# Where x is loaded around the projection of a two-layer kernel: three tiles in the last attention head, layer 1's tiles during the projection

## The chip, the cores and the metric

The kernel runs on one core of one Trainium2 chip. The metric is the device time of one execution in microseconds (us), taken as the median over runs. A profile of one further execution, with its hardware trace, is there as well; its instants are us from the start of the span.

## What is computed

The input x is one image of 48 channels and 256 x 256 pixels in float32. Two layers are applied, each with a group norm in front and a residual around it:

```
x = x + L0(groupnorm(x))     # attention over patches
x = x + L1(groupnorm(x))     # channel, column and row mixing in 64 x 64 windows

L0: qkv = 3x3 depthwise conv of (w_qkv applied to the channels)
    patches of 4 x 4, stride 4, padding 4; 8 heads of 96 features
    q, k scaled to unit length; attn = softmax(q k * temperature)
    out = v times attn, folded back to pixels, then w_proj over the channels
L1: out = sum over t < 3 of einsum('bcphqw,twW,thH,tcC->bCpHqW', x in windows, Ws, Hs, Cs)
```

There are 4096 patches inside the image; the padding patches enter the softmax as a constant.

## The kernel before

**Attention.** After a first stage (group statistics, the 1x1 convolution of the first two heads, the depthwise convolution of head 0) one long stretch runs under `tc.manual_schedule()`: each engine gets its instructions in the order of the text. It loops over 8 heads `h` and 16 blocks `g`. In each block PE makes scores (L337), ACT exponentiates them (L566), PE weighs the values (L595, in four parts `k`), and DVE accumulates into `oacc` (L606). While head `h` runs, the `Depthwise` objects prepare head `h + 1`; their tiles (`pad`, `acc`, `o` and others), and those of the strips of the 1x1 convolution, lie in the pool `cv`, about 50 KB a partition. In the last head nothing is left to prepare, but `cv` is held to the end, by `attention.close()`. SP loads the keys, queries and values; `load_query` (L311) fills one of two buffers for the block after next.

`store(h, m)` (L608 to L618) transposes a part of `oacc`, copies it to `oo` on ACT (two buffers, in the pool `asm`), and POOL stores it to `os_` in DRAM. The last head's eight stores are spread over the last block, and the last two come at its very end.

**Projection.** Then a loop over 8 tiles `t` of 16 rows of each half of the image follows, outside the manual schedule, so the order of instructions is planned by the framework. For each tile SP loads `pot` from `os_` (L740) and `pxt`, the same rows of x, from the input (L741), two DMAs of 768 KB each; the two pools have three buffers each. PE applies `wp` (L746), DVE adds into `pxt` (L753) and takes the statistics for the second group norm (L757), and POOL stores `pxt` to `x1s` in DRAM (L762). After the loop, a chain of small operations (L764 to L788) makes `csn` and `cbias` out of the statistics: the channel weights of layer 1 with the norm folded in.

**Layer 1.** A second manual schedule works in units of 64 rows by 128 columns. `load_x(u)` (L815) reads `lxq` from `x1s`, with the channels on partitions; `load_rows(u)` (L824) reads `lrt` from `x1s`, with the rows on partitions, for the residual. `over_c` applies `csn` (L841, DVE writes `lzt` at L848), `over_w` (L863) and `over_h` (L880) follow, and POOL stores the result. The tiles `lxq` lie in the pool `lx` (three buffers), opened after the projection's pools are closed, on the memory that these held. Units 0 and 1 are asked for first thing:

```
for u in range(2):
    load_x(u)
for _ in over_c(0):
    pass
```

Of the kernel before, what the change touches and what calls it, by code (L numbers as in the profile page):

```python
# [8 lines left out]
F32 = mybir.dt.float32  # L9
# [4 lines left out]
PSUM = bass.MemoryType.PSUM  # L14
DRAM = bass.MemoryType.DRAM

C = 48
H = W = 256
HALF = H // 2
P2 = 2 * C  # L20
KS = 4
KK = KS * KS
NH = 8
HD = C * KK // NH
# [9 lines left out]
PX = W // KS  # L34
# [5 lines left out]
TP = 256  # L40
T3 = 3
WS = 64
# [3 lines left out]
def conv_preact_kernel(  # L46
# [15 lines left out]
    nc = tc.nc  # L62
    xc = x.rearrange("b c y x -> (b c) y x")
# [15 lines left out]
    x1s = dram.tile([C, H, W], F32, name="x1s")  # L79
# [18 lines left out]
    for s in range(2):  # L98
        r = slice(s * C, (s + 1) * C)
        for h in range(NH if s == 0 else H0):  # L100
            o = s * M0 + h * HC if h < H0 else (h - H0) * HC
            nc.gpsimd.dma_start(
                out=(wq[r] if h < H0 else wr[0:C])[:, o : o + HC].rearrange("c (z e) -> c z e", z=3),
                in_=w_qkvT.rearrange("c (z h e) -> h c z e", z=3, h=NH)[h],
# [373 lines left out]
                nc.sync.dma_start(out=rows, in_=ot[s * M0 : (s + 1) * M0])  # L478

    attention = ExitStack()  # L480
    cv = attention.enter_context(tc.tile_pool(name="cv", bufs=1))
    one = attention.enter_context(tc.tile_pool(name="one", bufs=2, space=PSUM))

    ots = [cv.tile([M1, 4, W + 2], F32, name=f"ot{i}") for i in range(NOT)]
# [39 lines left out]
    with tc.tile_pool(name="ahead", bufs=2) as ah, tc.tile_pool(name="ae", bufs=3) as ae, tc.tile_pool(  # L524
        name="asm", bufs=6
    ) as asm, tc.tile_pool(name="ao", bufs=1) as ao, tc.tile_pool(name="big", bufs=3, space=PSUM) as big:
        MB = 8
        NK = NB // MB
        NG = NB // G
        keys, queries, values, oaccs = {}, {}, {}, {}  # L530

# [76 lines left out]
        def store(h, m):  # L608

            pt = one.tile([HD, 4, 128], F32, name="pt", tag="one")  # L610
            for i in range(4):
                nc.tensor.transpose(pt[:, i, :], oaccs[h, m // 2][:, m % 2, i * HD : (i + 1) * HD], ident)  # L612
            oo = asm.tile([HD, 512], F32, name="oo", bufs=2)
            nc.scalar.copy(oo, pt.rearrange("p i n -> p (i n)"))  # L614
            for i in range(512 // TP):
                nc.gpsimd.dma_start(  # L616
                    out=os_[m * (512 // TP) + i, h * HD : (h + 1) * HD, :], in_=oo[:, i * TP : (i + 1) * TP]
                )  # L618
# [16 lines left out]
        with tc.manual_schedule():  # L635
            load_query(0, 1)
            block = scores(0, 0)
            for h in range(NH):
                more = h + 1 < NH
                rows = {r: Depthwise(h + 1, r) for r in range(CR + 1)} if more else {}  # L640
                for g in range(NG):
                    p, d, n = rows.get(g - 2), rows.get(g - 1), rows.get(g)

                    if h == 0 and 0 < g <= 6:
                        load_value(0, g + 1)
                    if more and CR + 2 <= g < CR + 6:
                        for m in range(2):
                            load_value(h + 1, (g - CR - 2) * 2 + m)
                    if more and CR + 3 <= g < CR + 6:
                        for m in range(2):  # L650
                            load_key(h + 1, (g - CR - 3) * 2 + m)

                    blocks = [normalised(*block)]
                    if p:
                        p.norm()
                        p.root()
                    block = scores(h, g * G + 1)
                    if more and g == NG - 1:
                        load_key(h + 1, 6)
                        load_key(h + 1, 7, nc.gpsimd)  # L660
                    if g + 2 < NG:
                        load_query(h, g + 2)
                    elif more:
                        load_query(h + 1, g + 2 - NG)
                    if p:
                        p.scale()
                    if d:
                        for t in range(1, 4):
                            d.tap(t)
                    second = block  # L670
                    if g + 1 < NG:
                        block = scores(h, (g + 1) * G)
                    elif more:
                        block = scores(h + 1, 0)
                    blocks.append(normalised(*second))
                    if d:
                        for t in range(4, 9):
                            d.tap(t)

                    if g == 0 and rows:  # L680
                        rows[0].load()

                    if h == 0 and 0 < g <= 6:
                        turn(0, g + 1)
                    if more and CR + 2 <= g < CR + 6:
                        for m in range(2):
                            turn(h + 1, (g - CR - 2) * 2 + m)
                    if g == 0 and h > 0:
                        for m in range(6, 8):
                            store(h - 1, m)  # L690
                    if p:
                        p.patches()
                        p.store((2,))
                        p.high()
                    if d:
                        d.square()
                    if n:
                        n.first()
                    for k in range(NK):
                        s = (h * NG + g) * NK + k  # L700
                        weigh(h, g, blocks, k)
                        if k == 0 and d:
                            d.reduce()
                        if k == 0 and p:
                            p.low(nc.gpsimd)
                            p.store((0, 1))
                        if s % 2:
                            for w in strips[s - 1] + strips[s]:
                                w.run(big.tile([128, 2, 512], F32, name="big"))
                            for w in strips[s + 1] + strips[s + 2]:  # L710
                                w.load()
                        elif s:
                            for w in strips[s - 2] + strips[s - 1]:
                                w.store()
                        if k == 2 and g + 1 in rows:
                            rows[g + 1].load()

                        if g == NG - 1 and k > 0:
                            for m in range(2 * k - 2, 2 * k):
                                store(h, m)  # L720
            for m in range(6, 8):
                store(NH - 1, m)
# [1 line left out]


    l1c = ctx.enter_context(tc.tile_pool(name="l1c", bufs=1))
    RP = TP // PX * KS
    NP = TP
    with tc.tile_pool(name="pj", bufs=3) as pj, tc.tile_pool(name="pjs", bufs=1) as pjs, tc.tile_pool(
        name="pps", bufs=3, space=PSUM  # L730
    ) as pps, tc.tile_pool(name="pp1", bufs=1, space=PSUM) as pp1:
# [1 line left out]
        ov = os_.rearrange("t (c k) n -> t c k n", k=KK)  # L733
        for t in range(HALF // RP):
            ot = pj.tile([P2, KK, NP], F32, name="pot")
            xt = pj.tile([P2, RP, W], F32, name="pxt")
            for s in range(2):
                r = slice(s * C, (s + 1) * C)
                y0 = s * HALF + t * RP
                nc.sync.dma_start(out=ot[r], in_=ov[s * (NT // 2 // TP) + t])  # L740
                nc.sync.dma_start(out=xt[r], in_=xc[:, y0 : y0 + RP, :])  # L741
            xv = xt.rearrange("p (py ki) (px kj) -> p ki kj py px", ki=KS, kj=KS)
            for ki in range(KS):
                ps = pps.tile([P2, KS, NP], F32, name="pps")
# [15 lines left out]
            for s in range(2):  # L760
                y0 = s * HALF + t * RP
                nc.gpsimd.dma_start(out=x1s[:, y0 : y0 + RP, :], in_=xt[s * C : (s + 1) * C])  # L762

        gm2 = pjs.tile([P2, 64 + C], F32, name="gm2")  # L764
        nc.vector.memset(gm2, 0.0)
# [20 lines left out]
        nc.tensor.matmul(pb1, lhsT=mrow, rhs=csn[0:C], start=True, stop=True)  # L786
        cbias = l1c.tile([128, T3 * C], F32, name="cbias")
        nc.vector.tensor_copy(cbias, pb1)  # L788


    with tc.tile_pool(name="lx", bufs=3) as lx, tc.tile_pool(name="lz", bufs=2) as lz, tc.tile_pool(
        name="lr", bufs=2
    ) as lr, tc.tile_pool(name="ly", bufs=4) as ly, tc.tile_pool(name="ps1", bufs=2, space=PSUM) as ps1, tc.tile_pool(
        name="ps2", bufs=2, space=PSUM
    ) as ps2, tc.tile_pool(name="ps3", bufs=1, space=PSUM) as ps3:
        wsb = lz.tile([128, T3, 128], F32, name="wsb", bufs=1)
# [2 lines left out]
        for s in range(2):  # L799
            r = slice(s * WS, (s + 1) * WS)  # L800
            nc.scalar.dma_start(out=wsb[r, :, r], in_=Ws.rearrange("t w v -> w t v"))
            nc.scalar.dma_start(out=hsb[r], in_=Hs.rearrange("t h g -> h t g"))
        HW = WS // 2
        units = [(yw, xh) for yw in range(H // WS) for xh in range(2)]
        NQ = 3
        xqs, rts, zts, blks, parts = {}, {}, {}, {}, {}

        def load_x(u):

            yw, xh = units[u]  # L810
            xcol = slice(xh * 128, (xh + 1) * 128)
            xq = lx.tile([64 + C, HW, 128], F32, name="lxq")
            for s in range(2):
                y0 = yw * WS + s * HW
                nc.sync.dma_start(out=xq[s * 64 : s * 64 + C], in_=x1s[:, y0 : y0 + HW, xcol])  # L815
            xqs[u] = xq

        def load_rows(u):

# [80 lines left out]


        with tc.manual_schedule():
            for u in range(2):
                load_x(u)
            for _ in over_c(0):
                pass
            late = None
# [57 lines left out]
```

## Time and profile before

| | |
|---|---|
| median of 3 runs | 3701.59 us |
| lowest, highest | 3696.06, 3705.06 us |
| profiled execution | 3698.24 us, its span 3696.2 us |
| busy: PE, DVE, ACT, POOL | 94%, 58%, 51%, 15% of the span |
| last head | about 2860 to 3210 |
| last stores of attention, first projection matmul | 3210 to 3239 |
| projection, first matmul to last statistics | 3239 to 3380 |
| statistics chain and wait for layer 1's x | 3380 to 3400 |
| layer 1 | 3400 to 3696 |
| DMA | 386.48 MB, 105 GB/s over the span |

Busy times are of instructions at work; PE's weight loads overlap its matmuls. "SPq" names the DMAs that SP issues, with the time that the issue took. A DMA share of 1 means that the core's 16 DMA engines were all busy. Releasers of waits ("<-") are inferred from semaphore events.

### The profile page before, as it was taken

What the parts mean: (1) busy time and instruction counts of PE and PEld (TensorE: products, weight loads), DVE (VectorE), ACT (ScalarE), POOL (GpSimd) and SP (SyncE); (2) the same over time, 40 slices, a digit from 0 to 9 for tenths busy, and PEclk for the clock granted to TensorE, in tenths of its full rate; (3) what the DMA queues carried; (4) which work ended last, traced back from release to release, by engine and by line L of the source; (5) the groups of instructions that cost most, each with busy time, mean ns of one, the idle gap of its engine ahead of it and who ended that gap; (6) DMA issues with size and microseconds to landing.
All of it is one profiled execution on the core that took longest, in us unless ns stands there. A gap on an engine that the chain in (4) does not pass through costs nothing.

```text
span 3696.2 us, 100318 instructions
## 1 busy us (share of the span) xinstructions
PE 3466.8 (94%) x44252; PEld 2905.8 (79%) x44252; DVE 2139.4 (58%) x3514; ACT 1873.3 (51%) x2747; POOL 542.9 (15%) x628
## 2 busy tenths in 40 slices
PE   2869999999999999999999999999999999855998
PEld 1337777898888898988888989888889888713776
DVE  5454774189628953894399349925982222266654
ACT  0235676566546654665566556655664444300332
POOL 2030111012111211121122112201220000000011
PEclk9989999999999999999999999999999999966999
DMA  7455666533323332333233323332333100299774
GB/s 160 152 133 153 176 170 171 149 96 95 94 79 82 93 89 75 83 90 96 73 92 86 87 73 93 86 87 84 94 79 87 36 19 19 51 248 197 127 138 92
DMA packets 274146, 386.48 MB, mean 105 GB/s; under 512 B 77010, under 2 KB 211522, under 8 KB 269480
## 3 DMA queue, kind: packets, MB, share of 16 engines
q1 hardware_dynamic: 234790, 264.95, 27.4%
q0 software_dynamic: 35424, 106.40, 12.4%
q10 hardware_dynamic: 3490, 8.64, 1.1%
q8 instruction: 350, 5.73, 0.7%
q14 instruction: 92, 0.75, 0.1%
HBM read 234.76 MB, written 144.90 MB: 103 GB/s over the span
## 4 chain that ended last, share of the span: by engine, by line
PE 82%; DMA 6%; DVE 2%; issue 1%; SPq 1%; ACT 1%; ACTq 0%; POOL 0%; POOLq 0%; DVEq 0%
PE big L337 36%; PE big L595 35%; PE pb L863 4%; PE pa L841 2%; PE pc L880 2%; DMA pxt<-in_x_dram 2%; DMA t<-ot 1%; PE big L177 1%; DVE acc L228 1%; PE pt L612 1%; DMA pad<-t 1%; PE pn L247 1%; DMA pot<-os__70 1%; PE pst L549 1%; DMA x1s<-pxt 0%
## 5 line engine op out<-in xcount | busy, mean ns | idle before, releaser
L566 ACT ACTIVATE e<-big,nmx 128x1024 f32<-128x1024 f32 x1024 | 1143.8, 1118 | 875.5 <-PE big L337 613.1
L337 PE MATMUL big<-kt,qt 128*128 128x512 f32 x6144 | 1436.7, 392 | 31.1 <-DMA kt<-qkv 29.0
L595 PEld LDWEIGHTS big<-vn,e 128*64 128x64 f32 x32768 | 1357.0, 137 | 57.2 <-ACT e L566 30.6
L595 PE MATMUL big<-vn,e 128*64 128x96 f32 x32768 | 1387.3, 247 | 6.1 <-DVE oacc L606 2.5
L337 PEld LDWEIGHTS big<-kt,qt 128*128 128x128 f32 x6144 | 1144.6, 188 | 279.6 <-issue 28.8
L606 DVE TENSOR_TENSOR oacc<-big,oacc 128x768 f32<-128x768 f32 x480 | 453.4, 954 | 713.0 <-PE big L595 713.0
L228 DVE SCALAR_TENSOR_TENSOR acc<-pad,dwt,acc 126x1024 f32<-126x1024 f32 x592 | 765.5, 1293 | 39.8 <-ACT acc L209 24.0
L295 POOL DMA_DIRECT2D qkv<-o x72 | 52.8, 734 | 1240.7 <-ACT o L279 1240.7
L579 DVE TENSOR_REDUCE zt<-zs 128x1 f32<-128x4 f32 x256 | 38.4, 150 | 335.1 <-ACT e L566 335.1
L289 POOL TENSOR_TENSOR ol<-o,oh 126x1024 fp32r<-126x1024 f32 x78 | 184.9, 2370 | 311.1 <-DVE ss L243 237.8
L566 ACT ACTIVATION_READ_ACCUMULATOR e<-big,nmx 128x1 f32 x1024 | 196.3, 192 | 0.0
L848 DVE TENSOR_TENSOR lzt<-pa,cbias 128x864 f32<-128x864 f32 (+1 forms) x88 | 137.0, 1628 | 96.4 <-PE pa L841 96.4
L870 ACT COPY lyt<-pb 128x512 f32<-128x512 f32 x144 | 84.5, 587 | 212.4 <-PE pb L863 212.4
L279 ACT COPY o<-acc 126x1024 f32<-126x1024 f32 x74 | 159.1, 2150 | 0.0
L863 PEld LDWEIGHTS pb<-wsb,lzt 128*64 128x64 f32 x2304 | 126.1, 138 | 27.6 <-issue 19.5
L616 POOL DMA_DIRECT2D os__70<-oo x128 | 65.2, 515 | 541.6 <-ACT oo L614 541.3
L863 PE MATMUL pb<-wsb,lzt 128*64 128x128 f32 x2304 | 142.0, 279 | 1.3 <-issue 1.3
L746 PE MATMUL pps<-pot,wp 96*96 96x512 f32 x128 | 79.1, 787 | 61.5 <-DMA pot<-os__70 61.5
L239 ACT ACTIVATE sq<-acc 126x1024 f32<-126x1024 f32 x74 | 78.2, 1057 | 100.7 <-DVE acc L228 100.7
L180 ACT ACTIVATE ot<-big,bias 108x1024 f32<-108x1024 f32 x64 | 68.2, 1111 | 113.1 <-PE big L177 71.4
L209 ACT ACTIVATE acc<-pad,dwt 126x1024 f32<-126x1024 f32 x74 | 84.1, 1137 | 80.6 <-DMA pad<-t 80.6
L746 PEld LDWEIGHTS pps<-pot,wp 96*96 96x96 f32 x128 | 26.9, 219 | 113.3 <-issue 79.0
(124 smaller groups left out, 1977.0 us busy)
## 6 DMA issues: line engine op xcount, KB each, us to landing
pad<-t SPq DMA_DIRECT2D x238, 254.0 KB
t<-ot SPq DMA_DIRECT2D x128, 217.7 KB
qkv<-ol POOLq DMA_DIRECT2D x78, 336.0 KB, 6.1
qkv<-oh POOLq DMA_DIRECT2D x70, 336.0 KB, 5.6
qt<-qkv SPq DMA_DIRECT2D x176, 96.0 KB
xs<-in_x_dram SPq DMA_DIRECT2D x128, 96.0 KB
os__70<-oo POOLq DMA_DIRECT2D x128, 96.0 KB, 2.1
pxt<-in_x_dram SPq DMA_DIRECT2D x16, 768.0 KB
```

Source lines behind the costliest of these rows:

```text
L209: nc.scalar.mul(self.acc, self.pad[:, 0:KS, 0:W], dwt[:, self.h, 0:1])
L228: nc.vector.scalar_tensor_tensor(self.acc, self.pad[:, dy : dy + KS, dx : dx + W], dwt[:, self.h, tap : tap + 1], self.acc, ALU.mult, ALU.add,
L279: nc.scalar.copy(self.o.rearrange("p (a b) x -> p a b x", a=KS), self.acc.rearrange("p a (x b) -> p a b x", b=KS))
L289: eng.tensor_sub(self.ol, self.o, self.oh.bitcast(F32))
L337: nc.tensor.matmul(ps[:, i, :], lhsT=qt[:, r, q0 : q0 + 128], rhs=kts[2 * j + i][:, r // 2, :], start=(r == 0), stop=(r == 2),)
L566: nc.scalar.activation(e[:, j * 1024 : (j + 1) * 1024], ps.rearrange("p a b -> p (a b)"), AF.Exp, bias=nmx[:, b : b + 1], accum_out=zs[:, ...
L595: nc.tensor.matmul(ps[p : p + 64, j // 4, j % 4 * HD : (j % 4 + 1) * HD], lhsT=e[:, mb * 128 + p : mb * 128 + p + 64], rhs=vn, start=(i == 0),
L606: nc.vector.tensor_add(oaccs[h, k], ps[:, :, : 4 * HD], oaccs[h, k])
L746: nc.tensor.matmul(ps[:, i : i + 2, :], lhsT=wp, rhs=ot[:, ki * KS + i : ki * KS + i + 2, :], start=True, stop=True,)
L848: nc.vector.tensor_tensor(zv[:, :, y0 : y0 + n, :], pa[:, :, : n * T3 * C].rearrange("p s (y k) -> p s y k", y=n), cbias.rearrange("p (u v ...
L863: nc.tensor.matmul(pb[s * WS : (s + 1) * WS, i, :], lhsT=zts[u][:, t * C + c + i, :], rhs=wsb[:, t, :], start=True, stop=True,)
L870: nc.scalar.copy(yt[:, t, :], pb.rearrange("p i x -> p (i x)"))
```

## The change

The pool `cv` gets a stack of its own, `convolution`, on the right-hand side of the memory, and is closed at the start of the last head. A pool `pe` takes its place. It holds three tiles `xts` of x, for the projection's tiles 0 to 2, and one more buffer of `oo`, for the very last store. The x tiles are loaded by SP in blocks 1 to 6 of the last head, in the parts k = 1 and k = 3 of each, with two DMAs of 4 rows of a half (192 KB) each time, 24 in all. The projection loads x only for t >= 3.

The pool `lx` is opened ahead of the projection's pools, so it shares no place with them, and `load_x` for units 0 and 1 moves from the head of layer 1 to the end of the projection's loop. `pe` is closed after `cbias`.

```
+    convolution = ExitStack()
+    cv = convolution.enter_context(tc.tile_pool(name="cv", bufs=1, side="right"))
+    NX = 3
...
+            late = h == NH - 1 and m >= NM - NLATE
+            oo = (pe if late else asm).tile([HD, 512], F32, name="oo", bufs=NLATE if late else 2)
...
+                    if not more and g == 0:
+                        convolution.close()
+                        early = ExitStack()
+                        pe = early.enter_context(tc.tile_pool(name="pe", bufs=1, side="right"))
+                        xts = [pe.tile([P2, RP, W], F32, name=f"xt{t}") for t in range(NX)]
...
+                        if not more and 0 < g <= 2 * NX and k in (1, 3):
+                            i = (g - 1) * 2 + k // 2
+                            t, y = i // 4, i % 4 * (RP // 4)
+                            for half in range(2):
+                                y0 = half * HALF + t * RP + y
+                                nc.sync.dma_start(
+                                    out=xts[t][half * C : (half + 1) * C, y : y + RP // 4, :],
+                                    in_=xc[:, y0 : y0 + RP // 4, :],
+                                )
...
+    lx = ctx.enter_context(tc.tile_pool(name="lx", bufs=3))
...
-            xt = pj.tile([P2, RP, W], F32, name="pxt")
+            xt = xts[t] if t < NX else pj.tile([P2, RP, W], F32, name="pxt")
...
-                nc.sync.dma_start(out=xt[r], in_=xc[:, y0 : y0 + RP, :])
+                if t >= NX:
+                    nc.sync.dma_start(out=xt[r], in_=xc[:, y0 : y0 + RP, :])
...
+        for u in range(2):
+            load_x(u)
...
+    early.close()
...
         with tc.manual_schedule():
-            for u in range(2):
-                load_x(u)
             for _ in over_c(0):
```

More of the change, by code (lines that the diff above doesn't have):

```diff
@@ L480, in conv_preact_kernel @@
     attention = ExitStack()
-    cv = attention.enter_context(tc.tile_pool(name="cv", bufs=1))
+    convolution = ExitStack()
+    cv = convolution.enter_context(tc.tile_pool(name="cv", bufs=1, side="right"))
+    NX = 3
     one = attention.enter_context(tc.tile_pool(name="one", bufs=2, space=PSUM))
@@ L528, in conv_preact_kernel @@
         NK = NB // MB
+        NLATE = 1
+        RP = TP // PX * KS
         NG = NB // G
@@ L612, in store @@
                 nc.tensor.transpose(pt[:, i, :], oaccs[h, m // 2][:, m % 2, i * HD : (i + 1) * HD], ident)
-            oo = asm.tile([HD, 512], F32, name="oo", bufs=2)
+            late = h == NH - 1 and m >= NM - NLATE
+            oo = (pe if late else asm).tile([HD, 512], F32, name="oo", bufs=NLATE if late else 2)
             nc.scalar.copy(oo, pt.rearrange("p i n -> p (i n)"))
@@ L726, in conv_preact_kernel, with load_x @@
     l1c = ctx.enter_context(tc.tile_pool(name="l1c", bufs=1))
-    RP = TP // PX * KS
     NP = TP
+    lx = ctx.enter_context(tc.tile_pool(name="lx", bufs=3))
+    HW = WS // 2
+    units = [(yw, xh) for yw in range(H // WS) for xh in range(2)]
+    xqs = {}
+    def load_x(u):
+        yw, xh = units[u]
+        xcol = slice(xh * 128, (xh + 1) * 128)
+        xq = lx.tile([64 + C, HW, 128], F32, name="lxq")
+        for s in range(2):
+            y0 = yw * WS + s * HW
+            nc.sync.dma_start(out=xq[s * 64 : s * 64 + C], in_=x1s[:, y0 : y0 + HW, xcol])
+        xqs[u] = xq
     with tc.tile_pool(name="pj", bufs=3) as pj, tc.tile_pool(name="pjs", bufs=1) as pjs, tc.tile_pool(
@@ L788, in conv_preact_kernel @@
         nc.vector.tensor_copy(cbias, pb1)
-    with tc.tile_pool(name="lx", bufs=3) as lx, tc.tile_pool(name="lz", bufs=2) as lz, tc.tile_pool(
-        name="lr", bufs=2
-    ) as lr, tc.tile_pool(name="ly", bufs=4) as ly, tc.tile_pool(name="ps1", bufs=2, space=PSUM) as ps1, tc.tile_pool(
+    early.close()
+    with tc.tile_pool(name="lz", bufs=2) as lz, tc.tile_pool(name="lr", bufs=2) as lr, tc.tile_pool(name="ly", bufs=4) as ly, tc.tile_pool(name="ps1", bufs=2, space=PSUM) as ps1, tc.tile_pool(
         name="ps2", bufs=2, space=PSUM
@@ L802, in conv_preact_kernel @@
             nc.scalar.dma_start(out=hsb[r], in_=Hs.rearrange("t h g -> h t g"))
-        HW = WS // 2
-        units = [(yw, xh) for yw in range(H // WS) for xh in range(2)]
         NQ = 3
[L806 to L816, printed above, removed]
+        rts, zts, parts = {}, {}, {}
         def load_rows(u):
```

## The prediction

> **What bounds the kernel now.** The page comes first: PE is busy 94% of the span, but its 40 slices dip near the end, and the DMA digits rise to 9 there. The change touches only that stretch, so I read it by windows (columns: length, PE, PEld, DVE, ACT, POOL busy, PE clock, DMA share, GB/s).
>
> ```profile
> DMA  7455666533323332333233323332333100299774
> 2980.00:3040.00 60.00, 60.00 (x786) 53.14 (x784) 13.80 (x34) 28.94 (x48) 0.00 (x0) 1.00 0.08 22
> 3222.00:3239.00 17.00, 3.92 (x39) 3.09 (x35) 0.96 (x1) 4.08 (x7) 6.05 (x12) 0.70 0.80 171
> 3252.00:3272.00 20.00, 10.44 (x16) 3.52 (x16) 17.18 (x20) 0.00 (x0) 2.04 (x4) 0.69 1.01 257
> 3290.00:3308.00 18.00, 10.32 (x16) 3.52 (x16) 12.51 (x12) 0.00 (x0) 1.01 (x2) 0.69 1.00 262
> 3344.00:3362.00 18.00, 9.05 (x16) 3.05 (x16) 12.33 (x12) 0.00 (x0) 1.01 (x2) 0.78 1.01 269
> 3362.00:3380.00 18.00, 10.09 (x16) 3.41 (x16) 12.55 (x13) 0.00 (x0) 1.01 (x2) 0.69 0.45 129
> 3386.00:3393.00 7.00, 0.18 (x1) 0.00 (x0) 0.69 (x2) 0.00 (x0) 0.00 (x0) 0.50 1.18 162
> 3475.00:3510.00 35.00, 35.00 (x500) 26.23 (x492) 21.48 (x15) 10.56 (x18) 4.17 (x6) 1.00 0.79 141
> ```
>
> Three stages show. The last head (row 2980) is PE's alone, DMA at 0.08. The projection (rows 3252 to 3344) is bound by the DMA engines: share 1.0, about 262 GB/s, while PE works 10 and DVE 12.5 of 18 us per tile. In layer 1 (row 3475) PE is full again. Ahead of the projection (row 3222) and behind it (row 3386) PE stands nearly idle; the timeline gives the ends of the second gap:
>
> ```profile
> 3339.57 0.42 SPq L741 DMA_DIRECT2D pxt<-in_x_dram  x1
> 3362.70 10.09 PE L746 MATMUL pps<-pot,wp 96*96 96x512 f32 x16 [9.04 <-DMA pot<-os__70]
> 3379.89 1.88 DVE L130 BATCH_NORM_AGGREGATE mv<-st 96x2 f32<-96x384 f32 x1
> 3384.66 11.16 SPq L815 DMA_DIRECT2D lxq<-x1s  x4
> 3386.22 0.31 DVE L788 COPY cbias<-pb 128x144 f32<-128x144 f32 x1 [0.61 <-PE pb L786]
> 3393.05 0.81 PE L841 MATMUL pa<-csn,lxq 48*128 48x144 f32 x2 [6.87 <-DMA lxq<-x1s]
> 3398.37 3.22 PE L841 MATMUL pa<-csn,lxq 48*128 48x144 f32 x22 [4.50 <-DMA lxq<-x1s]
> 3400.18 3.08 DVE L848 TENSOR_TENSOR lzt<-pa,cbias 128x864 f32<-128x864 f32 x2 [13.01 <-PE pa L841]
> ```
>
> The statistics end at T = 3379.9. cbias is ready 6.6 us later, but DVE's first lzt comes 20.3 us after T, because lxq is asked for only at 3384.66. SP's own waits say why, and one early DVE line shows how the untied part of the program is ordered:
>
> ```profile
> SPq L741 <- DMA x1s<-pxt: 81.2, 5, 22.4
> SPq L815 <- DMA x1s<-pxt: 44.2, 2, 28.1
> SPq L740 <- DMA os__70<-oo: 21.5, 3, 10.9
> 3210.50 0.15 DVE L765 MEMSET gm<- 96x112 f32 x1 [0.64 <-DVE vn L585]
> ```
>
> SP stood 44.2 us in front of lxq for stores of x1s, although unit 0 needs only rows 0 to 63, the first four tiles of one half. It waited for the last tile's stores: for lxq's place, which the projection's pool held. And the memset of L765, written behind the tile loop, ran at 3210, before it: what is ready is put forward.
>
> **What the Trainium skill says.** "DMA: Bandwidth & Descriptors", section "Issuing engines are not separate DMA queues", says that transfers issued by SP, ACT and GpSimd share the same 16 engines. The trace agrees: SP's loads and POOL's stores together fill the share to 1.0. Its "Specifications" give 512 B as enough for line rate; here the measurement decides: lxq and lrt move 512 B pieces (128 columns of f32) and reach 141 to 205 GB/s at a share above 1, the projection's longer pieces 262. "TensorE: Matmul & The Clock Gate", Part 1, says that an idle PE falls to half clock; the trace shows 0.50 from 3380 to 3420. I expect that ramp again, only earlier.
>
> **The change part by part.** One half-tile is 768 KB, so pot, x and the x1s store of a tile are 1.573 MB each.
>
> *x in the last head.* 24 loads of 192 KB over blocks g = 1 to 6. On SP they stand behind load_query(g+2) in each block. A block is 21.8 us; four issues at about 0.41 us (pxt's median) are 1.7 us, and 768 KB at 262 GB/s 2.9 us. From 2830 to 3200 SP spent 271.2 us in 17 waits for PE before query loads, and a query asked for in the middle of block g is needed a block later: of the 21.8 us its nine or so issues of 0.43 us and the landing (2 to 3 us, estimated from the 2.1 of os) take 7, so some 15 are spare. Cost 0; uncovered it would be 4.6 us a block. Their place is that of cv, whose last tenant, head 7's convolution, ended a head earlier. Moving cv itself to the other side costs 0 plus or minus 2 us.
>
> *Start of the projection.* Before, the first x loads (3210) ran against the os stores: the oo copies waited up to 7.0 us for their buffers, and the second half of pot was asked for at 3232.41. The stores' usual landing is 2.1 us. Without x in the way, and with the last oo in its own buffer, m = 4 lands near 3227 and PE begins near 3233 instead of 3238.9. The new lx moves pot over keys and e, last used by 3223, and the later x tiles over oacc and oo, free near 3230: neither is later than pot's data. Gain 6 (2 to 8).
>
> *The DMA-bound middle.* From 3238.9 to the last tile's first matmul at 3362.7 are 123.8 us, for 7 tiles of loads (22.0 MB) and about six tiles of stores (9.4 MB): 254 GB/s. Two x tiles leave this stretch (the first had landed before it): 28.3 MB, 111.4 us. Gain 12.4. With DVE at 12.5 us a tile it stays DMA's.
>
> *Layer 1's loads.* Units 0 and 1 are 3.15 MB. At the 144 GB/s of 3384 to 3407 they cost 21.9 us, at the best windows' 203 GB/s 15.5; I take 18.5. All depends on where they enter SP's queue. They are ready when tile 3 is stored, just when SP stands before the x of tile 6 or 7 for its buffer (the 81.2 us). As L765 went forward, so I expect these four to go in front of the last x loads. Then they take their 18.5 us from the saturated engines before the last tile lands. SP's four issues, up to 5.2 us each in layer 1, hold back the loads behind them, while the engines stay busy.
>
> *The gap.* With lxq there, over_c begins when csn, cbias and the place of lzt are ready. That place is still the projection's and waits for the last x1s store, landed by T + 4.7 before; DVE's wsb memset waits with it. First lzt near T + 8 instead of T + 20.3: gain 12.3 (8 to 13). Behind it nothing changes: over_c(0) at half clock, then PE-bound units; the lrt loads move forward with it.
>
> Sum: 6 + 12.4 - 18.5 + 12.3 = 12.2 us. The profiled execution took 3698.24 (span 3696.2); that leaves 3686.0. The median of the three runs lies 3.35 above it, so 3689.4.
>
> **The rivals.** *A, the lxq loads stay behind the last tile.* They then use the tail, where the share is 0.45. T falls by 18.4; lxq shares the engines with the last x1s store, so lzt starts near T + 10: gain 10. Sum 28.4, median 3673. For it: the order of the text, and x and pot of one tile keep it in the trace. Against: L765.
>
> *B, the change doesn't do what it says:* the waits for x1s are for its data, not for the place, and are not by rows. The trace shows waits by part for os (first pot at 3221.21, later stores from 3222) but cannot tell for x1s. Then only the 18.4 remain: 3683. If instead the 512 B pieces cost 30 us inside the full engines, nothing remains: 3701.
>
> *C, slower: the last head's cover fails.* If the x loads hold the queries back, PE waits in six blocks: 6 x 4.6 = 27.6 us against a gain of 12.2, 15 slower, 3717. It decides once a query lands over 15 us later than now. Against it: heads 0 to 6 run at shares of 0.3 with PE full.
>
> **How the numbers follow.** Forecast 0.56, with a range of its own of 3682 to 3697; A 0.18; B 0.13; C, with any other loss, 0.13. Within 0.3% (11 us, about what a measurement of this kernel can tell from no change) lies a little less than half of the forecast, since 12.2 is barely above it, and B's costly end: 0.30. Faster 0.57, slower 0.13. The range, 3668 to 3708, reaches past A and leaves most of C out.
>
> **What would show it.** Right: PE full from 2920 to 3210 with DMA share near 0.15; four lxq issues before the last pxt; T within 5 us of 3380 and first lzt 8 us after it; no SP wait of L815 at 3340. Wrong: T near 3361 with lxq last (A); lxq after T (B); idle PE in L337 for qt (C).

## The result and the profile after

The changed kernel takes 3677.03 us (median of 4 runs, 3676.36 to 3681.3) against 3703.24 us for the kernel before in the same comparison. The ratio is 0.9934, with a 95% interval from 0.9918 to 0.995: some 24 us, between 18 and 30. The profiled execution took 3676.93 us, its span is 3674.8 us, 21.4 us below the span before.

The page's row of the DMA share, in 40 slices, now shows the last head's x loads as a 2 and a 2 ahead of the empty stretch, and the slices of the projection as 0, 8, 9 instead of 2, 9, 9:

```profile
DMA  7455666533323332333233323332333220089774
```

The windows of the changed kernel (length, PE, PEld, DVE, ACT, POOL busy, PE clock, DMA share, GB/s):

```profile
2980.00:3040.00 60.00, 60.00 (x820) 53.69 (x815) 14.79 (x36) 26.32 (x44) 0.00 (x0) 1.00 0.19 52
3236.00:3247.00 11.00, 0.00 (x0) 0.00 (x0) 0.00 (x0) 0.00 (x0) 0.00 (x0) 0.50 0.96 184
3260.00:3272.00 12.00, 7.85 (x12) 2.66 (x11) 11.97 (x12) 0.00 (x0) 0.74 (x2) 0.72 1.01 225
3345.00:3360.00 15.00, 5.37 (x7) 1.99 (x8) 9.34 (x11) 0.00 (x0) 1.00 (x2) 0.56 1.02 239
3372.00:3380.00 8.00, 4.28 (x27) 4.02 (x29) 4.42 (x14) 0.41 (x2) 0.00 (x0) 0.50 1.00 274
3455.00:3490.00 35.00, 35.00 (x504) 26.70 (x502) 21.45 (x15) 10.54 (x18) 4.17 (x6) 1.00 0.81 141
```

In the last head (2980) PE is as full as before while x comes in beside it, at a share of 0.19. In the first tiles (3260) DVE is busy 11.97 of 12 us. The DMA engines are full as well, but with loads for later tiles: for a while DVE sets the pace. The engines stay full to 3380, past the last tile, because layer 1's loads now lie there. New is the row at 3236: 11 us in which no compute engine does anything.

The timeline of the changed kernel has the ends of the stages:

```profile
3212.59 0.27 DVE L591 TENSOR_SCALAR vn<-vT,rz 128x96 f32<-128x96 f32 x1
3235.81 20.83 SPq L776 DMA_DIRECT2D pot<-os__70  x7
3247.14 14.32 PE L783 MATMUL pps<-pot,wp 96*96 96x512 f32 x28 [16.41 <-DMA pot<-os__70]
3330.15 0.42 SPq L778 DMA_DIRECT2D pxt<-in_x_dram  x1
3330.67 39.48 SPq L762 DMA_DIRECT2D lxq<-x1s  x4
3354.63 10.04 PE L783 MATMUL pps<-pot,wp 96*96 96x512 f32 x16 [9.73 <-DMA pot<-os__70]
3371.77 1.89 DVE L130 BATCH_NORM_AGGREGATE mv<-st 96x2 f32<-96x384 f32 x1
3378.09 0.31 DVE L827 COPY cbias<-pb 128x144 f32<-128x144 f32 x1 [0.61 <-PE pb L825]
3379.68 3.08 DVE L874 TENSOR_TENSOR lzt<-pa,cbias 128x864 f32<-128x864 f32 x2
```

The last vn (the values divided by the softmax sum; L591, L585 before) is the end of the scores' part of attention and a good zero for what follows. From it the table below is made, for this pair and for the experiments: **start** is from the last vn to the first projection matmul, **middle** from there to the last tile's first matmul, **tail** from there to the end of the statistics (L130), **gap** from there to the first lzt, **rest** to the end of the span. All are us of one profiled execution each.

| | last vn | start | middle | tail | gap | rest | sum from vn | ratio to before (95%) |
|---|---|---|---|---|---|---|---|---|
| before | 3209.6 | 29.3 | 123.8 | 17.2 | 20.3 | 296.0 | 486.6 | 1 |
| changed | 3212.6 | 34.6 | 107.5 | 17.1 | 7.9 | 295.1 | 462.2 | 0.9934 (0.9918 to 0.995) |
| e1 x only | 3219.6 | 29.0 | 103.6 | 16.6 | 20.9 | 295.3 | 465.5 | 0.9957 (0.9944 to 0.997) |
| e2 layer 1 only | 3207.4 | 35.3 | 132.6 | 17.7 | 7.9 | 295.3 | 488.9 | 0.9984 (0.9973 to 0.9994) |
| e3 own pot pool | 3211.1 | 29.5 | 109.2 | 17.1 | 7.8 | 295.3 | 458.8 | 0.9912 (0.9898 to 0.9927) |
| e4 lxq in front | 3209.8 | 33.3 | 129.9 | 17.2 | 7.8 | 296.6 | 484.8 | 1.0006 (0.9995 to 1.0016) |
| e5 pools in order | 3210.1 | 35.3 | 101.8 | 16.6 | 9.4 | 295.7 | 458.8 | 0.9908 (0.9892 to 0.9923) |
| e6 and reuse | 3219.2 | 34.7 | 107.7 | 17.5 | 7.7 | 295.0 | 462.6 | 0.9903 (0.9888 to 0.9919) |
| e7 place only | 3210.8 | 34.7 | 105.2 | 16.4 | 10.2 | 295.4 | 461.9 | 0.9917 (0.9904 to 0.9931) |
| e8 e5, four oo | 3217.2 | 31.7 | 101.3 | 17.6 | 10.0 | 296.6 | 457.3 | 0.99 (0.9885 to 0.9916) |
| e9 e3, four oo | 3219.0 | 28.2 | 104.2 | 17.1 | 7.8 | 297.2 | 454.5 | 0.9911 (0.9896 to 0.9927) |
| e10 cv to the right | 3221.5 | 32.8 | 124.1 | 16.2 | 20.7 | 295.1 | 488.8 | 1.001 (1.0 to 1.0019) |

The first column moves by up to 14 us from kernel to kernel for reasons that were not found (see e10), so the stages are compared from vn on. Between the pair shown: start +5.3, middle -16.3, tail -0.1, gap -12.4, rest -0.9, and vn itself 3.0 later; in all -21.4.

### The profile page after: what moved, and what is told of

Its sections match the earlier page's. It is cut to its first block, busy times and chain, and to the rows that moved or that the text cites. A ratio compares the mean times of both kernels' runs of the same rounds, so it can differ in the third digit from the quotient of the medians.

```text
span 3674.8 us, 100335 instructions
## 1 busy us (share of the span) xinstructions
PE 3466.3 (94%) x44252; PEld 2908.2 (79%) x44252; DVE 2138.7 (58%) x3514; ACT 1872.6 (51%) x2747; POOL 541.8 (15%) x628
## 4 chain that ended last, share of the span: by engine, by line
PE 83%; DMA 4%; DVE 3%; issue 1%; SPq 1%; ACT 1%; POOL 0%; POOLq 0%; ACTq 0%; DVEq 0%
PE big L337 37%; PE big L601 36%; PE pb L889 4%; PE pa L867 2%; PE pc L906 2%; DMA pxt<-in_x_dram 1%; DVE acc L228 1%; PE big L177 1%; PE pt L618 1%; PE pn L247 1%; PE pst L555 1%; DMA pad<-t 0%; DVE xt L790 0%; DMA kt<-qkv 0%; DMA x1s<-pxt 0%
## 5 line engine op out<-in xcount | busy, mean ns | idle before, releaser
L337 PEld LDWEIGHTS big<-kt,qt 128*128 128x128 f32 x6144 | 1147.8, 189 | 278.4 <-issue 28.4
L228 DVE SCALAR_TENSOR_TENSOR acc<-pad,dwt,acc 126x1024 f32<-126x1024 f32 x592 | 765.6, 1293 | 39.5 <-DMA pad<-t 19.1
L585 DVE TENSOR_REDUCE zt<-zs 128x1 f32<-128x4 f32 x256 | 38.5, 150 | 336.6 <-ACT e L572 336.6
L243 DVE TENSOR_REDUCE ss<-sq 126x64 f32<-126x1024 f32 x80 | 97.4, 1219 | 25.6 <-ACT sq L239 25.6
```

The source lines that it names most:

```text
L228: nc.vector.scalar_tensor_tensor(self.acc, self.pad[:, dy : dy + KS, dx : dx + W], dwt[:, self.h, tap : tap + 1], self.acc, ALU.mult, ALU.add,
L243: nc.vector.tensor_reduce(self.ss, self.sq.rearrange("p a (x b) -> p x a b", b=KS), AX.XY, ALU.add)
L337: nc.tensor.matmul(ps[:, i, :], lhsT=qt[:, r, q0 : q0 + 128], rhs=kts[2 * j + i][:, r // 2, :], start=(r == 0), stop=(r == 2),)
```

## The experiments

The theory after the result, called P: the DMA engines bound everything from the first pot load to the last tile; when they can begin is decided by the *place* of pot. SP's waits in the changed kernel show a single one of 64.8 us ahead of the first pot load:

```profile
SPq L776 <- DMA os__70<-oo: 64.8, 1, 64.8
SPq L778 <- DMA x1s<-pxt: 32.5, 2, 19.3
```

Before, three waits for os stores came to 21.5 us, and loads went out in between as their parts arrived. From the timeline of the kernel before:

```profile
3210.05 0.79 SPq L741 DMA_DIRECT2D pxt<-in_x_dram  x2
3221.21 11.97 SPq L740 DMA_DIRECT2D pot<-os__70  x3
3238.89 1.99 PE L746 MATMUL pps<-pot,wp 96*96 96x512 f32 x2 [6.76 <-DMA pot<-os__70]
```

Now no pot load is issued until 3235.81, 1.8 us after the last store was issued, and then six at once. The new lx had pushed the projection's pool upwards, onto oo and oacc. The rival, D: the waits are for the stores' data.

**e1: x alone.** lx is opened, and units 0 and 1 are asked for, where they were before:

```
-    lx = ctx.enter_context(tc.tile_pool(name="lx", bufs=3))
-        for u in range(2):
-            load_x(u)
...
+    with tc.tile_pool(name="lx", bufs=3) as lx, tc.tile_pool(name="lz", bufs=2) as lz, ...
+            for u in range(2):
+                load_x(u)
             for _ in over_c(0):
```

> One part of the change alone: x of tiles 0 to 2 in the last head (with the last oo in its own buffer), while layer 1's pool lx and its loads stay where they were before. Theory P (place): in the changed kernel pot waits for the last oo store because its pool, pushed up by lx, lies on the attention's small tiles; here lx does not push it, so pot is asked for as its parts are stored, PE starts about 24 us after the last vn (before 29.3, changed kernel 34.6), the middle (first projection matmul to the last tile's first matmul) takes about 108 us (before 123.8), and the gap from the last statistics to the first lzt stays at 20.3. Sum: 20 us faster than before, ratio 0.9945. Rival D (data): pot waits for the stores themselves, now later, whatever the place; then PE starts 34.6 us after vn as in the changed kernel, and the gain is 16.3 - 5.3 = 11 us, ratio 0.997.

From vn to the end 21.1 us were saved in the profiled execution, with start 29.0 and gap 20.9, as P had it; the middle is even shorter, 103.6. The runs give 0.9957, 16 us (11 to 21): in this execution vn came 10 us late. The start agrees with P, not with D (34.6). It is not shorter than before, though: 24 us were expected, 29.0 came.

**e2: layer 1's part alone.** `NX = 0`, no `pe`, cv on the left again; lx and load_x as changed:

```
-    convolution = ExitStack()
-    cv = convolution.enter_context(tc.tile_pool(name="cv", bufs=1, side="right"))
+    cv = attention.enter_context(tc.tile_pool(name="cv", bufs=1))
+    NX = 0
```

> The other part alone: lx has its own place and units 0 and 1 are asked for behind the projection's loop; no x in the last head, cv on the left as before. Theory P: projection as before (PE start 29.3 us after vn, middle 123.8), since the pool of pot and pxt here lies on keys and e, not on oo; lxq comes last on SP, uses the tail, and the gap falls from 20.3 to about 8 us: 12 us faster, ratio 0.9967. If lxq takes its 18.5 us (the price of the prediction) from the last tiles' loads all the same, the middle grows by it, and the ratio is 1.0015 or so.

The gap fell to 7.9 as expected, but the start grew by 6 us and the middle by 9, so that only 0.9984 remains. SP's queue shows the reason for the start:

```profile
3222.47 0.30 SPq L769 DMA_DIRECT2D pot<-os__70  x1
3222.82 0.42 SPq L771 DMA_DIRECT2D pxt<-in_x_dram  x1
3236.46 0.30 SPq L769 DMA_DIRECT2D pot<-os__70  x1
```

Before, both halves of pxt for tile 0 were asked for at 3210.05, 0.5 us after vn, because the pool lay on cv and keys, which nobody used any more. Here lx takes the lowest place, that of cv (both near 50 KB), and the pool of pot and pxt is pushed up until it reaches from the keys onto e. The first x goes out 15.4 us after vn, behind the last weighing, and its second half later still. The middle's 9 us are half in the first tile, which had come nearly complete before, and half in tiles of 19 us instead of 18. The tiles run at 19 us from the second one on, long before lxq is asked for (3350.91), so these loads are not the cause; what is stays open. So even this part alone costs the projection, in the start and the first tile through a place, most of what it saves in the gap.

**e3: pot in its own pool.** The changed kernel with two lines changed:

```
+    with tc.tile_pool(name="po", bufs=3) as po, tc.tile_pool(name="pj", bufs=3) as pj, ...
-            ot = pj.tile([P2, KK, NP], F32, name="pot")
+            ot = po.tile([P2, KK, NP], F32, name="pot")
```

> The changed kernel, but pot in a pool of its own, opened ahead of pxt's, so that its place lies on keys, values and e only and not on oo and oacc. Theory P: the first pot load is asked for right after the last weighing (14 us or so after the last vn instead of 23.2), PE starts about 27 us after vn instead of 34.6, the engines' idle time ahead of it is used, and the whole gains 7 us more than the changed kernel: ratio to before about 0.9915. Rival D: nothing changes, 0.9934.

The timeline of e3:

```profile
3226.12 24.64 SPq L776 DMA_DIRECT2D pot<-os__70  x7
3240.58 3.70 PE L783 MATMUL pps<-pot,wp 96*96 96x512 f32 x4 [5.58 <-DMA pot<-os__70]
```

The first pot load goes out 15.0 us after vn (3211.1) instead of 23.2, and PE starts after 29.5 instead of 34.6. Not an address of pot has moved, only the pool's bounds: the wait was for the place of the whole pool, and D falls. The ratio, 0.9912, is what was expected (0.9915), but its interval overlaps the changed kernel's. In the traces the 5.1 us of the start are partly lost again in the middle (109.2 instead of 107.5), and from vn on e3 is 3.4 us faster than the changed kernel: that the place held pot back is shown, a gain of 7 or 8 us in the whole is not.

**e4: layer 1's loads in front.** The order that the forecast had assumed, made by hand:

```
+            if t == 6:
+                for u in range(2):
+                    load_x(u)
...
-        for u in range(2):
-            load_x(u)
```

> The changed kernel, but units 0 and 1 of layer 1 are asked for ahead of tile 6's loads, the order that the prediction had taken for likeliest. If its price holds (18.5 us of full DMA engines ahead of the last tile), the last statistics come 18.5 us later than in the changed kernel and only the tail's contention is saved: ratio to before about 0.998. Rival: the engines were busy with these loads before the end anyway (the changed kernel shows a share of 1.0 up to 3380), so that only part of the price is lost, about 8 us: ratio 0.9955.

Nothing remains of the gain: 1.0006. From e4's timeline:

```profile
3285.90 41.40 SPq L762 DMA_DIRECT2D lxq<-x1s  x4
3327.40 7.29 SPq L779 DMA_DIRECT2D pot<-os__70  x1
3355.85 10.16 PE L786 MATMUL pps<-pot,wp 96*96 96x512 f32 x16 [33.34 <-DMA pot<-os__70]
```

SP is held for 41.4 us by four issues, tile 6's loads follow at 3327, and PE stands 33.3 us. Meanwhile the DMA engines stay full (columns as above):

```profile
3295.00:3345.00 50.00, 19.01 (x32) 6.57 (x32) 28.02 (x30) 0.00 (x0) 2.01 (x4) 0.64 1.09 258
```

The middle is 22.4 us longer than in the changed kernel. The price of the prediction (18.5) was of the right kind and 4 us short; the rival, that only some 8 us of it would be lost, falls. With this order, the forecast's own, the change as a whole gains nothing.

**e5 and e6: use the idle stretch too.** In the changed kernel the DMA share is 0.15 and 0.34 in the two dozen us after vn. e5 opens the attention's pools as oo and oacc, keys and values, e, and gives pxt a pool ahead of pot's, so that pxt stands on keys alone:

```
+    with tc.tile_pool(name="asm", bufs=6) as asm, tc.tile_pool(name="ao", bufs=1) as ao, tc.tile_pool(
+        name="ahead", bufs=2) as ah, tc.tile_pool(name="ae", bufs=3) as ae, ...
...
+    with tc.tile_pool(name="pj", bufs=3) as pj, tc.tile_pool(name="po", bufs=3) as po, ...
```

> The changed kernel with the attention's pools opened in another order (oo and oacc at the bottom, then keys and values, then e) and with pxt in a pool ahead of pot's, so that pxt for tiles 3 to 5 lies on keys and values alone, free at the last vn, and pot lies on e, free at the last weighing. Theory P, that place decides when the full DMA engines begin: x of tiles 3 to 5 moves in the idle stretch before the projection (three half-tiles or so are asked for at the last vn); PE starts at about 29 us after vn, as before, but the middle shrinks to about 98 us (109 with pot's own pool): 18 to 20 us less than the changed kernel less what the os stores lose, ratio to before about 0.989. Rival: the early x loads slow the oo stores as they did before the change, the start slips by what the middle gains, and the ratio stays at 0.991.

The middle fell to 101.8 and the start rose to 35.3: the rival. From e5's timeline:

```profile
3210.54 1.25 SPq L778 DMA_DIRECT2D pxt<-in_x_dram  x3
3227.90 1.07 ACT L621 COPY oo<-pt 96x512 f32<-96x512 f32 x2 [10.43 <-DMA os__70<-oo]
3235.96 1.07 ACT L621 COPY oo<-pt 96x512 f32<-96x512 f32 x2 [7.00 <-DMA os__70<-oo]
```

Three loads of x fill the engines right after vn, and the oo copies wait 10.4 and 7.0 us for stores that share these engines. That is the kernel before's own trouble, brought back. From vn on, e5 and e3 take the same 458.8 us.

e6 also lets tiles 6 and 7 use the buffers of tiles 0 and 1:

```
-            xt = xts[t] if t < NX else pj.tile(...)
+            xt = xts[t % 6] if t % 6 < NX else pj.tile(...)
```

> The kernel of e5, but x of tiles 6 and 7 goes into the buffers of tiles 0 and 1, free early, instead of those of tiles 3 and 4. It takes away SP's waits for the x1s stores of tiles 3 and 4. If these waits leave the DMA engines idle, the middle shortens by 5 us or more; if the engines are full anyway (theory: bytes decide), nothing changes against e5 within 2 us.

SP's two waits for x1s ahead of tiles 6 and 7 (27.7 us in e5, 32.5 in the changed kernel) are gone, and nothing is won: 0.9903 against 0.9908, and a middle that is 6 us longer in the trace, not within 2 us. A window of e5 and one of e6, in the later tiles of the projection:

```profile
3290.00:3330.00 40.00, 22.37 (x39) 7.18 (x38) 34.28 (x35) 0.00 (x0) 3.01 (x6) 0.72 1.01 285
3305.00:3345.00 40.00, 18.78 (x32) 6.19 (x32) 30.63 (x32) 0.00 (x0) 3.01 (x6) 0.73 1.01 259
```

The engines are full in both, so taking the waits away freed nothing. That they move fewer bytes in e6 at the same share goes with its longer middle; why is not shown.

**e7: the place without the early request.** load_x goes back to the head of layer 1, lx keeps its place:

```
-        for u in range(2):
-            load_x(u)
...
+            for u in range(2):
+                load_x(u)
             for _ in over_c(0):
```

> The changed kernel with lx in its own place, but units 0 and 1 asked for at the head of layer 1, as before the change. It tells apart two reasons why the projection's tiles ran at 19 us each in the changed kernel and at 17.2 to 18 with x alone moved: if the early lxq loads cost it, tiles run at 17.5 us and the middle is 104 us; if the place of pot and pxt costs it, tiles stay at 19 and the middle at 107 us. The gap: if lxq's place alone made it wait, it could be asked for as soon as SP comes to it, behind the last pxt, since the queue has nothing else; then the gap is 8 us even so, and the ratio 0.993 to 0.994. If the order of the text holds it behind the statistics, the gap stays near 20 and the ratio is about 0.996.

```profile
3326.54 0.42 SPq L778 DMA_DIRECT2D pxt<-in_x_dram  x1
3327.06 40.10 SPq L762 DMA_DIRECT2D lxq<-x1s  x4
```

SP comes to lxq as soon as its last pxt is out, 0.5 us later, exactly as in the changed kernel. So of layer 1's part the place does the work, and the move of the request does nothing that can be measured (0.9917, interval overlapping the changed kernel's). The gap is 10.2, not 8: the memset of wsb, just ahead of the first lzt, waits 3.2 us for DMAs here and 0.9 in the changed kernel. The later tiles ran at 18.1 to 18.7 us, in the changed kernel, with the same places and the same lxq issues, at 18.7 to 19.1, and there at 18.7 already in tile 4, before the first lxq issue. So neither of the two reasons that e7 was to tell apart is shown; the rate differs between executions.

**e8 and e9: four oo buffers.** Two of them lie in pe, and copies 2, 3, 6 and 7 of the last head use them:

```
-        NLATE = 1
+        NLATE = 2
-            late = h == NH - 1 and m >= NM - NLATE
+            late = h == NH - 1 and m % 4 >= 2
```

> The kernel of e5, where the early x loads made the oo copies wait 10.4 and 7.0 us for their two buffers, with four oo buffers in the last head (two of them beside the early x tiles). If these waits are what ate e5's gain, the second and third pair of copies no longer wait for the pair just ahead, the last os store is issued 8 us earlier after the last vn (31.5 us in e5), PE starts at 27 to 29 us instead of 35.3, and the ratio to before falls from 0.991 to about 0.989. Rival: PE starts when pot's bytes have come through the engines that the x loads filled, whatever oo does; the start stays at 34 to 35 us and the ratio at 0.991.

> The kernel of e3 with the same four oo buffers. There no x load stands in the stores' way, and the copies waited 2 to 3 us at most, so 2 us at most are to be had: ratio 0.9905 to 0.9915, start 27.5 to 29.5 us after the last vn.

e8's start is 31.7 instead of 35.3, between the two expectations, and the ratio 0.99 is not distinguishable from e5's. e9 has the shortest way from vn to the end of all (454.5), and yet 0.9911, as e3. (A copy of e3 does wait longer than its expectation says: 5.7 us.) All of e3, e5, e6, e8 and e9 lie between 0.99 and 0.9912, better than the changed kernel by 8 to 13 us in their centres, but this is not shown as a gain over it: e7, whose SP queue does what the changed kernel's does, came to 0.9917 beside e5 and e6, and from vn on the five are between 0.4 us slower and 7.7 us faster than the changed kernel. Nor can they be ranked among themselves. I would take e3, the smallest edit.

**e10: cv on the other side, alone.** Kernel before, with `side="right"` for cv and nothing else, because vn came late in several kernels that have it:

> The kernel before, with cv moved to the right-hand side and nothing else. In the profiled executions so far, head 0 (from the load of key 7 of head 0 to that of head 1 on POOL) took 430.1 and 430.9 us in the two kernels with cv on the left, and 430.6 to 438.7, mean 434.5, in nine with cv on the right. If the side costs these 4 us, the ratio to before comes out near 1.001 from that alone, and head 0 near 434; but pot and pxt then lie on keys and e instead of cv and keys, so the x of tile 0 can no longer be asked for at the last vn, which cost the start 6 us in the kernel with layer 1's part alone: then 1.0025. If head 0 only scatters from execution to execution, the ratio is 1.000 to 1.0015, all of it from the start of the projection.

Ratio 1.001 (1.0 to 1.0019), some 4 us, and the start is 3.5 us longer: x of tile 0 goes out 13.7 us after vn, late as in e2. That fits the last expectation, but the first one had named the same ratio, and the runs cannot tell the two apart. Head 0 took 439.6 us in the profiled execution, the longest of all, but the runs leave no room for 10 us. Whether a part of the scatter belongs to the side stays open.

## Why the prediction was right or wrong

It said 12.2 us faster, and the gain is some 24. The forecast's own range, 3682 to 3697, does not hold 3677. What came is the order of loads of its rival A (28.4), which it had thought three times less likely, without A's gain at the start. The signs named in advance agree: lxq went out last, and the statistics came 11.1 us earlier after vn, where A had said 18.4 and the forecast hardly any change. That the wide range, 3668 to 3708, holds the time is owed to A's place in it. And that the forecast at least named a gain is in part luck: two of its terms were wrong in opposite directions, and with the order that it assumed, made by hand in e4, nothing is gained. Step by step:

- **x in the last head, cost 0: right.** From the load of the last key of head 7 to the last vn it took 358.7 us before and after. SP waited for PE ahead of the query loads for 256.0 us instead of 271.2; PE waited for no query, and rival C is out.
- **Start, 6 us gained: wrong; 5.3 us lost.** The sentence that failed is "neither is later than pot's data". It asked what the place of each tile waits for; pot waited for the place of its whole pool, up to the end of the last store from the old oo buffers. The forecast had them free "near 3230"; the first pot load went out at 3235.81. e3 gives 5 us back by separating the pools. But the 6 us did not come there either: the start is 29.5 in e3 and 29.0 in e1, against 29.3 before and some 23 in the forecast. Without x in the way the oo stores did get quicker in the changed kernel (the copies waited at most 2.5 us for their buffers). In e1 and e3 the first pot load goes out early, 15.0 us after vn, and a copy behind it waits 5.8 and 5.7 us, much as one did behind x before. Of the 14.5 us from e3's first pot load to its first matmul, 8.3 pass until the second half's store has landed and its load is asked for, and 6.2 until the bytes are there.
- **Middle, 12.4 us gained: right in kind, 16.3 measured.** It is the bytes of x that leave. Some of the surplus only answers the late start, when pot's first six loads went out together ahead of PE: with the start repaired (e3) the middle is 109.2, a gain of 14.6. That DMA bounds it throughout was too simple: in the first tiles DVE sets the pace, at 12.5 us each.
- **Layer 1's loads, 18.5 us lost: wrong, and this is the largest term.** The price was nearly right (e4: 22.4); the order was not. I had inferred from one memset that ran early that these loads would go in front of the last x loads. They stayed last, at 3330.67, and used the tail: the last tile began 24.5 us after its last load was issued, 23.1 before and 21.7 in e1, which has no such loads there. So by this measure they cost 3 us at most. They went out ahead of the last tile's stores (3367.28), so rival B is out. That what is ready is put forward was not wrong in itself: in e7 the same loads, written behind the statistics, are issued ahead of them, and before the change x of tile 0 goes out 11 us ahead of pot of tile 0 (so not all of x and pot kept the order of the text, as I had noted for rival A). But it does not say how far forward, and one memset was too little for that. Why the planner stops behind the last x load, these runs do not show.
- **Gap, 12.3 us gained: right, 12.4.** The first lzt comes 7.9 us after the statistics: cbias begins after 6.3, and then the memset of wsb waits 0.9 for the last x1s store.
- **Rest: right.** 296.0 and 295.1.

So the forecast's total came out half as large because a term of 18.5 us did not occur, partly made up by a start that was wrong by 11.3 us in the other direction. The Trainium skill says in "DMA: Bandwidth & Descriptors", section "Issuing engines are not separate DMA queues", that all issuing engines share the same 16 engines. e5 agrees: loads that SP issues hold up stores that POOL issues, by 10.4 and 7.0 us. e4 is another case: there the loads that wait stand in SP's own queue.

## What to carry to other kernels

A pool that is given a place of its own pushes every later pool onto other tenants: list, for each pool that moves, whose last access it now waits for, and take the pool's whole extent, not the tile's. In a stretch that the DMA engines bound, ask of each transfer what stands behind it in its queue, since the same 3.15 MB cost 3 us at most behind the last tile's loads and 22 us in front of tile 6's. A wait of SP need not cost anything while the engines are full (e6).

## What was not expected of the hardware

- SP's four issues of lxq, 768 KB each in pieces of 512 B, took 39.5 us behind the last x load in the changed kernel and 41.4 in e4, where the engines were full, but 11.2 us at the head of layer 1 before and 11.3 in e1. Most loads of the same size in longer pieces took 0.3 to 1 us. The second of the four took longest, and the view of waits gives that time to a store:

```profile
SPq L762 <- DMA x1s<-pxt: 26.9, 1, 26.9
```

But all that unit 0 reads had been stored by 3314, when x of tile 6 was loaded into the buffer of tile 3. So this store is not what the load needed. That the full engines hold the issue is the likelier reading; no run tests it alone.
- Head 0 took between 430 and 440 us in twelve profiled executions. Heads 1 to 6 took 358 to 362 us, each within 0.5 us in all twelve. What scatters in head 0 was not found, and it blurs differences of a few us between kernels.
